# One graph layer: the ends of the transformer layers, layer 0's queries and the last group in a new order

## Chip, cores, metric

The kernel runs on one core of a Trainium2 chip, as one launch. The metric is the device time in microseconds; the time of a kernel is the median of its runs. TensorE is called PE here (PEld: its weight loads), VectorE DVE, ScalarE ACT, GpSimd POOL, and SyncE SP, which starts most of the transfers.

## What is computed

6250 nodes of 256 features, 106,250 edges of 64 features, all in float32. After a LayerNorm, the nodes go through two branches that are added to x; then a routed block of 32 small experts is added, each node by the one expert with the highest router value.

```python
xn = layernorm(x)
# branch 1: a graph network
agg = segment_sum(edge_attr, src) / max(count, 1)
g = relu(concat([xn, agg, u]) @ gW1 + gb1) @ gW2 + gb2
# branch 2: four layers with linear attention, 8 heads of 32
for i in range(4):
    h = layernorm(y) * g1 + b1                     # y starts as xn
    q = softmax(h @ Wq * s, over the 32 of a head)
    k = softmax(h @ Wk * s, over all 6250 nodes)
    context = einsum('nd,ne->de', k, h @ Wv)       # per head
    y = y + (q @ context) @ Wo + bo
    h = layernorm(y) * g2 + b2
    y = y + gelu(h @ W1 + c1) @ W2 + c2            # 256 -> 1024 -> 256
x = x + g + y
z = layernorm(x)
e = argmax(z @ router_w.T + router_b)
out = x + relu(relu(z @ W1[e] + b1[e]) @ W2[e] + b2[e])
```

## The kernel before

**Tiles and groups.** Nodes lie in 49 tiles of 128; `group(g)` is four tiles, 512 nodes. There are NG = 13 groups; the last, group 12, has one tile of 106 nodes. X keeps all nodes in SBUF. `pairs(n)` is two tiles[...]. `bank()` (L69) hands out six banks in turn, and a bank must have been read before it is written again; the edge products have two of their own. The order of the instructions is written by hand: each engine runs its instructions in the order of the program.

**A layer's context.** The softmax of k runs over all nodes, so a layer is cut in two. First, group by group, `qk` (L410) makes the keys transposed (L419), takes the running maximum, the exponentials `ek` and their sums `l`, and then the queries, as two pairs (L453), with their softmax in `q` on DVE and ACT (L459 to L468). `context_t` (L472) transposes ek (L479) into `kt` and q (L487) into `qT`. `context` (L491) adds a group's keys times its normed nodes (L499) to `C`, rescaled by `alpha`. When all 13 groups are done, `context_out` (L514) divides C by l, transposes it (L523), multiplies by Wv (L532), keeps the diagonal heads (L535) and multiplies by Wo (L538): `M` (L539) is what a query row is multiplied with. Only then can `attn_out` (L177, product L184) of the next part begin, followed by `norm2`, `attn_out_t` (transposes through L135), `ff_in` (L202, Gelu on ACT at L212) and `ff_out` (L215).

**The loops.** Layer 0's keys and queries have a loop of their own (L550): for each group the transposes of the group before (`context_t`), two halves of the norms of later groups (`norms_b`, `norms_a`), `qk`, `context` of the group before, one step of the edges, and the transposes of the next group. Then for layers 0 to 2 a loop over the 13 groups runs the second part of layer l and the first part of layer l+1 together: `ff_in`, `attn_out_t` of the next group, `context_t` of the group before, `ff_out`, `norm1`, `context`, `attn_out` two groups ahead, `norm1_t`, `qk`, `norm2`. After the loop come `context_t` and `context` of group 12 and then `context_out`. Layer 3's second part runs in a last loop together with the graph branch (`graph_in`, `graph_hidden_t`, `graph_hidden`, `graph_out`) and the router (`choose`, `route`).

**The edges.** The sums of edge features by node are made by 208 steps (`edges`), spread over the loops by hand: a load of features and of source ids (`edge_load`, SP), a comparison on DVE (`edge_match`, L352), a product on PE (`edge_sum`, L365) and four indirect transfers with addition into four tables in DRAM by POOL (`edge_add`, L383).

**Weights.** Each of w1, w2, wqkv and wo has one buffer, loaded again for the next layer by SP when its last reader is done: `load_w1` and `load_w2` around the last group, `load_wqkv` after `context_out`. The graph branch's weights (gwx, gwe, gwu, gwo, L627 to L630) lie in SBUF that the layers' pools give back when their block ends; a product with gwu (L639) makes the graph bias before the last loop.

**Router and experts.** `route` (L754) counts the nodes of each expert and scatters the rows of a group to the expert's place in the DRAM table `xtab`, by one indirect transfer for each tile (L775) from the buffer `rows`, of which there is one. After the loop the 32 experts read their first 256 rows (`xg`, L852), and 12 further blocks of 128 rows are read by `other_load` (L936) after `blank_rows` (L923) has cleared the ends of the long lists by six indirect transfers (L925). `experts` runs 44 slots; the result of each tile is scattered to the output by POOL (`out_x`, L987), two a slot for the 32, one for each further block. After each such scatter a memset of one element (`spare`) stands on POOL; the scatters are declared free of dependences among each other.

## Time and profile before

| | us |
|---|---|
| median of three runs (2973.36 to 2979.73) | 2975.72 |
| the profiled execution's own time | 2972.65 |
| its span, first to last instruction | 2970.9 |
| granted TensorE clock, mean | 0.976 |
| layer 0, to its first ff_in product | 0 to 220.8 |
| layers' loops, to the last layer's first ff_in product | 220.8 to 2121.2 |
| last loop, with graph branch and router | 2121.2 to 2839.6 |
| experts, from their first load | 2839.6 to 2970.9 |

The profile is that of one execution; its sums are compared with that execution's own time. A page gives each engine's busy time, the span in 40 slices, the chain of work that ended last, and the costliest groups of instructions; the trace behind it answers questions about one stretch: a timeline of each engine with the idle time before an instruction and the engine that ended it, the waits of an engine, and windows with the granted clock. "L223" is line 223 of the kernel. In the chain that ended last, 87% of the span is PE, 7% DVE, 2% ACT.

### The profile page before, as it was taken

How to read it: one execution, taken by the hardware profiler on the slowest of the kernel's cores; microseconds unless marked ns; L12 is line 12 of the kernel's file. 1: busy time of each engine (PE TensorE's matmuls, PEld its weight loads, DVE VectorE, ACT ScalarE, POOL GpSimd, SP SyncE). 2: the span in 40 equal slices, each digit the busy share in tenths (PEclk: the TensorE clock that was granted, in tenths of full speed). 3: DMA queues.
4: the chain of work that ended last, by engine and by line, in shares of the span. 5: the costliest groups of instructions: out<-in, count | busy, mean ns of one | idle time of the engine just before them, and what ended most of it. 6: DMA issues, size and time to landing. Idle time of an engine off the chain costs nothing.

```text
span 2970.9 us, 36212 instructions
## 1 busy us (share of the span) xinstructions
PE 2849.9 (96%) x12594; PEld 2056.6 (69%) x12594; DVE 1536.1 (52%) x4194; ACT 1126.9 (38%) x1995; POOL 1458.1 (49%) x1108
## 2 busy tenths in 40 slices
PE   7989999999989999999899999999799999999977
PEld 5767777777766777777767777777566766765654
DVE  7874645555546464646455555544343543543453
ACT  6754343434334344343443434344223223223232
POOL 0445777777747777777746656454001001001057
PEclk9999999999989999999999999999899999999888
DMA  8234555655555555555734443231200101102152
GB/s 257 35 50 84 75 96 75 97 73 97 79 110 82 89 82 88 78 94 78 133 59 79 76 75 49 42 43 18 74 15 29 36 22 29 36 22 72 55 188 76
DMA packets 368983, 219.12 MB, mean 74 GB/s; under 512 B 265913, under 2 KB 333469, under 8 KB 368792
## 3 DMA queue, kind: packets, MB, share of 16 engines
q1 hardware_dynamic: 241832, 175.32, 22.9%
q0 software_dynamic: 126144, 40.61, 17.3%
q8 instruction: 102, 1.67, 0.2%
q14 instruction: 89, 0.73, 0.1%
q10 hardware_dynamic: 816, 0.79, 0.1%
HBM read 135.46 MB, written 85.49 MB: 74 GB/s over the span
## 4 chain that ended last, share of the span: by engine, by line
PE 87%; DVE 7%; ACT 2%; issue 2%; POOL 1%; DMA 1%; POOLq 0%; SPq 0%; ACTq 0%; DVEq 0%
PE mm L223 23%; PE mm L209 23%; PE seg L365 5%; PE mm L184 5%; PE mm L419 5%; PE mm L499 4%; PE mm L453 4%; PE mm L699 3%; PE mm L135 3%; PE mm L715 3%; PE mm L700 2%; PE mm L487 1%; PE mm L479 1%; POOL out_x L987 1%; PE mm L972 1%
## 5 line engine op out<-in xcount | busy, mean ns | idle before, releaser
L383 POOL DMA_INDIRECT tab<-s,row x831 | 1313.5, 1581 | 738.4 <-issue 352.8
L209 PE MATMUL mm<-hT,w 128*128 128x512 f32 (+1 forms) x1664 | 686.5, 570 | 5.8 <-ACT hid L212 4.0
L223 PE MATMUL mm<-w,hid 128*128 128x256 f32 (+1 forms) x3136 | 687.8, 380 | 0.0
L223 PEld LDWEIGHTS mm<-w,hid 128*128 128x128 f32 (+1 forms) x3136 | 592.5, 190 | 80.1
L209 PEld LDWEIGHTS mm<-hT,w 128*128 128x128 f32 x1664 | 301.3, 190 | 354.7 <-issue 321.9
L121 ACT ACTIVATE sd<-mv,eps 128x4 f32<-128x4 f32 (+1 forms) x117 | 34.8, 297 | 991.3 <-DVE mv L120 991.1
L225 DVE TENSOR_TENSOR X<-mm,X 128x512 f32<-128x512 f32 (+1 forms) x100 | 68.1, 681 | 632.1 <-PE mm L223 632.1
L775 POOL DMA_INDIRECT xtab<-rows,to x49 | 48.2, 984 | 643.1 <-DVE to L773 574.1
L212 ACT ACTIVATE hid<-mm,col 128x512 f32<-128x512 f32 (+1 forms) x416 | 249.1, 669 | 101.1 <-PE mm L209 98.8
L365 PEld LDWEIGHTS seg<-edge,eq 128*128 128x128 f32 x1662 | 207.2, 192 | 21.5 <-issue 17.2
L365 PE MATMUL seg<-edge,eq 128*128 128x66 f32 x1662 | 202.7, 270 | 0.0
L139 ACT ACTIVATE hT<-mm,col 128x512 f32<-128x512 f32 (+1 forms) x208 | 145.0, 748 | 142.1 <-PE mm L135 140.8
L184 PE MATMUL mm<-M,qT 128*128 128x256 f32 (+1 forms) x784 | 191.3, 400 | 2.3 <-DVE M L539 2.3
L419 PE MATMUL mm<-hT,wqkv 128*128 128x512 f32 (+1 forms) x416 | 183.5, 584 | 3.5 <-ACT hT L139 3.5
L499 PE MATMUL mm<-z,kt 128*128 128x256 f32 (+1 forms) x784 | 181.8, 385 | 0.2 <-ACT kt L481 0.2
L453 PE MATMUL mm<-wqkv,hT 128*128 128x256 f32 (+1 forms) x784 | 177.7, 379 | 0.0
L453 PEld LDWEIGHTS mm<-wqkv,hT 128*128 128x128 f32 (+1 forms) x784 | 148.4, 190 | 40.7 <-issue 22.5
L184 PEld LDWEIGHTS mm<-M,qT 128*128 128x128 f32 (+1 forms) x784 | 156.2, 201 | 27.4 <-DVE M L539 4.2
L499 PEld LDWEIGHTS mm<-z,kt 128*128 128x128 f32 (+1 forms) x784 | 147.4, 192 | 19.1 <-ACT kt L481 0.4
L135 PE MATMUL mm<-ident,z 128*128 128x128 f32 x882 | 124.8, 277 | 28.3 <-DVE z L127 16.9
L352 DVE TENSOR_TENSOR eq<-all,srcf 128x512 f32<-128x512 int32 x208 | 142.9, 687 | 3.1 <-DMA all<-in_srct 2.7
L379 DVE TENSOR_SCALAR a<-s,twice,dump 128x4 f32<-128x4 f32 x208 | 60.4, 291 | 154.4 <-ACT s L367 154.4
(209 smaller groups left out, 3310.5 us busy)
## 6 DMA issues: line engine op xcount, KB each, us to landing
all<-in_srct SPq DMA_DIRECT2D x207, 256.0 KB, 3.8
xtab<-zero SPq DMA_DIRECT2D x32, 1036.0 KB, 10.2
edge<-in_edge SPq DMA_DIRECT2D x207, 128.0 KB, 2.7
tab<-s,row POOLq DMA_INDIRECT x831, 3.3
xg<-xtab SPq DMA_DIRECT2D x32, 259.0 KB, 5.9
w<-in_w SPq DMA_DIRECT2D x8, 1024.0 KB, 13.8
tab<-zero SPq DMA_DIRECT2D x40, 162.5 KB, 4.9
tb<-tab SPq DMA_DIRECT2D x48, 130.0 KB, 4.1
```

What stands on the lines that cost most here:

```text
L135: nc.tensor.transpose(ps[:, j * P:j * P + r], z[j][:r, k * P:(k + 1) * P], ident[:r, :r])
L139: nc.scalar.activation(hT[:, k, :cnt], ps[:, :cnt], AF.Identity, bias=col[:, bcol + k:bcol + k + 1], scale=col[:, gcol + k:gcol + k + 1])
L184: nc.tensor.matmul(ps[:r, j, :], qT[:, k, c0:c0 + r], M[:, k, :], start=(k == 0), stop=(k == 1))
L209: nc.tensor.matmul(ps[:, :cnt], w[:, k, b * P:(b + 1) * P], h[:, k, :cnt], start=(k == 0), stop=(k == 1))
L212: nc.scalar.activation(hid[:, :cnt], ps[:, :cnt], AF.Gelu, bias=col[:, c:c + 1], scale=1.0)
L223: nc.tensor.matmul(ps[:r, j, :], hid[b][:, c0:c0 + r], w[:, b, :], start=(b == 0), stop=(b == NHB - 1))
L352: nc.vector.tensor_tensor(out=eq[:, :m], in0=ALL.pop(b)[:, :m], in1=srcf[:, t0:t0 + m].unsqueeze(2).to_broadcast([P, m, P]), op=ALU.is_equal)
L365: nc.tensor.matmul(ps[:, i, :], eq[:, i, :], e[:, i, :], start=True, stop=True)
L383: nc.gpsimd.indirect_dma_start(out=tabs[i], out_offset=bass.IndirectOffsetOnAxis(ap=row[:, i:i + 1], axis=0), in_=s[:, i, :DE + 1], in_off ...
L419: nc.tensor.matmul(ps[:, :cnt], w[:, k, c:c + P], h[:, k, :cnt], start=(k == 0), stop=(k == 1))
L453: nc.tensor.matmul(ps[:r, j * D:(j + 1) * D], h[:, k, (j0 + j) * P:(j0 + j) * P + r], w[:, k, :D], start=(k == 0), stop=(k == 1))
L499: nc.tensor.matmul(ps[:, b, :], kt[b][:r, j * P:(j + 1) * P], z[:r, j, :], start=(j == 0), stop=(j == n - 1))
```

## The change

- `qk` is split into `keys`, `queries` (one pair each) and `queries_norm`, and `context_t` into `keys_t` and `queries_t`. `keys` calls a function `then` after the ek exponentials and before the sums of l.
- Layer 0: the queries of the group before are transposed after the key product of the group, no longer before it; the loop runs over 12 groups, and group 12 is written out behind it.
- The loop of a layer runs over 12 groups. Group 11 makes only its keys in it. Group 12 is written out behind it: its `ff_in`, the key transposes and queries of group 11, `ff_out` with the bias added ahead, `norm1`, the context of group 11 in two halves, the keys and one query product of group 12.
- `context_last` replaces `context` of group 12 and `context_out`: C is scaled by alpha and 1/l before the last product is added, the steps go by half on banks of their own, one half's copies on ACT and one on DVE, and M is copied by ACT. Two transposes of queries are called in its gaps (`fill`).
- `attn_out_first` replaces `attn_out` and `norm2` of group 0 in layers 0 to 2: the bias is added before M is there, and the statistics run pair by pair. The last layer keeps the old functions.
- `ff_in` of a group of one tile puts four products into one bank.
- Group 12 uses buffers of other names: its hT1 lies in an "hT2" tile and its q in a "z2" tile.
- The pools of the graph branch wait for freed bytes tile by tile (`reuse_waits="tile"`); the first loads of x and of the tables stand ahead of the four graph weights on SP, and the graph bias is made after `ff_out` of group 0.
- The last loop runs over 12 groups; behind it group 12's steps are nested with the router of group 11, and a group of one tile has a "rows1" buffer.
- `blank_rows` declares its transfers free of dependences among each other, puts a memset of one element behind each, and is called at slot 12 in place of 14.

```diff
+        def attn_out_first(l):
+            i0, n, r, t0, cnt = group(0)
+            xs = [X[:r, i0 + j0:i0 + j0 + m, :] for j0, m in pairs(n)]
+            for x2 in xs:
+                nc.vector.tensor_tensor(out=x2, in0=x2, in1=BO[l][:r].unsqueeze(1).to_broadcast([r, 2, D]), op=ALU.add)
...
+            for (j0, m), x2 in zip(pairs(n), xs):
+                ps = bank().rearrange("p (j d) -> p j d", j=2)
+                for j in range(m):
+                    c0 = t0 + (j0 + j) * P
+                    for k in range(2):
+                        nc.tensor.matmul(ps[:r, j, :], qT[:, k, c0:c0 + r], M[:, k, :], start=(k == 0), stop=(k == 1))
+                nc.vector.tensor_tensor(out=x2, in0=ps[:r, :m, :], in1=x2, op=ALU.add)
+                for j in range(j0, j0 + m):
+                    nc.vector.bn_stats(out=st[:r, j, :], in_=X[:r, i0 + j, :])
+                    nc.vector.bn_aggr(out=mv[:r, j, :], in_=st[:r, j, :])
...
+            m = 4 if n == 1 else 1
+            for b0 in range(0, NHB, m):
                 ps = bank()
...
-            def context_out(l):
+            def context_last(l, fill):
...
+                for b in range(2):
+                    nc.vector.tensor_scalar(out=C[:, b], in0=C[:, b], scalar1=alpha[:, b:b + 1], scalar2=rl[:, b:b + 1],
+                                            op0=ALU.mult, op1=ALU.mult)
+                ps = [bank()[:, :D] for _ in range(2)]
+                for b in range(2):
+                    nc.tensor.matmul(ps[b], kt[b][:r, :P], Z1[g][:r, 0, :], start=True, stop=True)
+                    nc.vector.scalar_tensor_tensor(out=C[:, b], in0=ps[b], scalar=rl[:, b:b + 1], in1=C[:, b],
+                                                   op0=ALU.mult, op1=ALU.add)
...
+                for b in range(2):
+                    pt = [bank()[:, :P] for _ in range(2)]
                     for k in range(2):
+                        nc.tensor.transpose(pt[k], C[:, b, k * P:(k + 1) * P], ident)
+                    nc.scalar.activation(GT[:, 0, b * P:(b + 1) * P], pt[0], AF.Identity, bias=col[:, bc:bc + 1],
+                                         scale=col[:, gc:gc + 1])
+                    nc.vector.tensor_scalar(out=GT[:, 1, b * P:(b + 1) * P], in0=pt[1], scalar1=col[:, gc + 1:gc + 2],
+                                            scalar2=col[:, bc + 1:bc + 2], op0=ALU.mult, op1=ALU.add)
+                    if b == 0:
+                        fill[0]()
...
+                    nc.scalar.copy(M[:, b], ps[:, :D])
+                fill[1]()
...
-            for g in range(NG):
+            for g in range(NG - 1):
                 if g:
-                    context_t(g - 1)
...
+                    keys_t(g - 1)
+                norms_b(g + 1)
...
+                def rest():
+                    if g:
+                        queries_t(g - 1)
+                    queries(0, g, 0)
+                    queries(0, g, 1)
+
+                keys(0, g, then=rest)
+                for i in range(2):
+                    queries_norm(g, i)
...
+            def last_steps(l):
+                g = NG - 2
+                queries_t(g, (0,), between=lambda: keys_t(g + 1))
+                context_last(l, (lambda: (queries_norm(g + 1, 0), queries_t(g, (1,))), lambda: queries_t(g + 1)))
...
+                ff_in(l, g + 1)
+                edges(2)
+                load_w1(n)
+                ff_bias(l, g + 1)
+                keys_t(g)
+                queries(n, g, 0)
+                queries(n, g, 1)
+                queries_norm(g, 0)
+                ff_out(l, g + 1, bias=False)
+                load_w2(n)
+                norm1(g + 1)
+                queries_norm(g, 1)
+                context(g, (0,))
+                norm1_t(n, g + 1)
+                context(g, (1,))
+                keys(n, g + 1, then=lambda: queries(n, g + 1, 0))
...
+                last_steps(n)
...
-            gw = gs.enter_context(tc.tile_pool(name="gw", bufs=1))
-            gp = gs.enter_context(tc.tile_pool(name="gp", bufs=1))
+            gw = gs.enter_context(tc.tile_pool(name="gw", bufs=1, reuse_waits="tile"))
+            gp = gs.enter_context(tc.tile_pool(name="gp", bufs=1, reuse_waits="tile"))
...
+            graph_load(0)
+            nc.sync.dma_start(out=gwx, in_=gw1[0:D, :].rearrange("(k p) h -> p k h", p=P))
...
-                rows = gp.tile([P, 4, XROW], F32, name="rows", bufs=1)
+                rows = gp.tile([P, n, XROW], F32, name="rows" if n > 1 else "rows1")
...
+            g = NG - 1
+            ff_in(l, g)
+            graph_in(g)
+            graph_out(g - 1)
+            graph_hidden_t(g)
+            ff_out(l, g)
+            graph_hidden(g)
+            choose(g - 1)
+            graph_out(g)
+            route(g - 1)
+            choose(g)
+            route(g)
...
+            tc.declare_no_dep(st.ins, group="blank", reason="rows of other experts")
+            tc.add_to_no_dep_group("blank", st.ins)
+            nc.gpsimd.memset(spare, 0.0)
...
-        elif s == 14:
+        elif s == 12:
             blank_rows()
```

## The prediction

> **What bounds the kernel.** I read the page's busy shares first, then PE's waits, then PE's timeline wherever it is not dense.

> ```profile
> PE 2849.9 (96%) x12594; PEld 2056.6 (69%) x12594; DVE 1536.1 (52%) x4194; ACT 1126.9 (38%) x1995; POOL 1458.1 (49%) x1108
> ...
> PEclk9999999999989999999999999999899999999888
> ```

> PE is busy 96% of 2970.9 us, so inside the layers' loops (one group of 512 nodes every 50.15 us, no gap in the timeline) an edit can win nothing. What can be won lies between the loops: the end of each layer's context, layer 0, and the router and experts at the end. PE's timeline at the end of the first full layer:

> ```profile
> 830.72 0.47 PE L479 MATMUL mm<-ident,ek 128*106 128x128 f32 x2
> 833.46 0.62 PE L487 MATMUL mm<-ident,q 106*128 106x106 f32 x2 [2.27 <-DVE q L468]
> 833.87 1.95 PE L499 MATMUL mm<-z,kt 106*128 106x256 f32 x4
> 837.67 1.09 PE L523 MATMUL mm<-ident,C 128*128 128x128 f32 x4 [1.85 <-DVE C L521]
> 839.47 2.10 PE L532 MATMUL mm<-kt,wqkv 128*128 128x128 f32 x8 [0.71 <-ACT kt L527]
> 842.09 2.07 PE L538 MATMUL mm<-wo,ek 128*128 128x256 f32 x4 [0.52 <-DVE ek L535]
> 844.94 9.55 PE L184 MATMUL mm<-M,qT 128*128 128x256 f32 x32 [0.78 <-DVE M L539]
> 855.77 1.64 PE L135 MATMUL mm<-ident,z 128*128 128x128 f32 x8 [1.27 <-DVE z L127]
> 857.84 2.41 PE L209 MATMUL mm<-hT,w 128*128 128x512 f32 x5 [0.43 <-ACT hT L139]
> ```

> Columns: start, duration, line, shapes, in brackets the idle time before it. For the last group (106 nodes) almost nothing but a chain runs: q normalized (2.27 idle), context, C scaled (1.85), transposes, V, heads, Wo, M (0.78), the attention product, the norm (1.27). Also, the same products take longer than elsewhere: 32 of L184 take 9.55 us, against 3.67 for 16 inside the loop. The granted clock, in windows of the same trace (us, busy PE, PEld, DVE, ACT, POOL, then PEclk):

> ```profile
> 832.70:849.80 17.10, 12.48 (x34) 9.03 (x35) 5.60 (x15) 2.89 (x6) 12.39 (x8) 0.50 0.84 183
> 203.40:206.80 3.40, 1.26 (x7) 0.70 (x6) 1.67 (x5) 0.92 (x2) 2.79 (x3) 1.00 0.34 18
> ```

> PE ran at half clock for 17.1 us there; in layer 0's end, where two products kept running through the gaps, it did not. Layer 0 and the last layer's start, from the waits:

> ```profile
> PE mm L487 <- DVE q L468: 20.0, 15, 2.3
> ...
> PE mm L639 <- DMA gwu<-in_gw: 5.7, 1, 5.7
> ```

> **The sum, part by part.** All durations are of the profiled execution.

> 1 *Layer boundary, twice (808.24 and 1445.74).* From the last key product of group 11 to the first ff_in product of the next layer is 857.84 - 808.24 = 49.6 us; the products in it, at full-clock durations of the loop, sum to 32.2. So 17.4 are waits and slow clock. The new order, walked from 808.24: ff_in of group 12 3.7 (in two banks instead of eight, so the 1.18 wait for ACT at L209 has no cause), edge products 2.5, key transposes 0.87, queries of group 11 3.45, ff_out 3.45, half the context 1.73: 824.05. The norm (add 0.42, stats 0.6, sqrt 0.3, scale 0.4, after ff_out's end at 822.3) is ready at 824.5, so 0.4 of wait; then transposes 0.2, half context 1.73, keys 0.92, query 0.86: 828.35. Now the chain: DVE and ACT for the key softmax end at 829.1, key transposes and copy 0.7, C scale on DVE until 830.8, product 0.43 and add 0.45 twice: 831.7; transposes 0.2 and copies 0.3 (ACT and DVE, a half each), with queries_norm's 1.1 on DVE in between, so that DVE's second half is done only at 833.4; V 0.43, heads 0.25, Wo 0.43, copy on ACT: M at 835.2. In the gaps run the query transposes (0.43, 0.18), which PE had before the chain. attn_out_first: two pairs 3.45, DVE add 0.7 and stats 1.1 for the second, sqrt 0.35, recip 0.2, first z 0.4..1.4, transposes, hT 0.7: ff_in at about 843.6, that is M + 8.4; attn_out(1) (3.45) lies beside it. 843.6 - 808.24 = 35.4. **14.2 us each, 28.4 for two.** The 128x256 copy on ACT has no row of its own; it lies between half of L481's (0.54 of a 1.08 pair, hence 0.3) and a whole one (0.54); I take 0.35. Behind that copy on ACT stand only the query copies (0.4), for which only attn_out of group 12 waits, 500 us later. The BO add now precedes M on DVE, under Wo.

> 2 *End of layer 0.* The same chain at full clock is 25.25 us today (195.59 to 220.84). New: keys 0.87, query 0.86, context of group 11 3.45, chain as above 14.9: 20.1. **5.2.**

> 3 *Layer 0.* Each group waits 1.1 us for q before L487; PE's work is 13.8 of 15.13. But DVE is nearly as full:

> ```profile
> 114.29 0.16 DVE L443 TENSOR_TENSOR l<-l,alpha 128x2 f32<-128x2 f32 x1 [0.24 <-ACT alpha L429]
> 115.62 0.16 DVE L444 TENSOR_TENSOR l<-l,ks 128x2 f32<-128x2 f32 x1 [1.18 <-ACT ek L439]
> ```

> DVE idles 1.42 of 15.13. The new order puts queries before the two sums of l, so both waits are covered by q's reductions; in exchange the q exponentials stand behind two qT copies (1.07) on ACT and DVE waits about 0.3 for them. Period 14.1, DVE-bound. It counts only from the edge match at 62.40, which waits for a load ("all", issued at 53.61 behind the 40 table clears on SP) and so stays put: eight periods, **7.4** (bounds 0 and 11).

> 4 *Last layer's start.* 2067.41 to 2121.16 is 53.75, with no edge products and 5.69 of wait for gwu. Chain as in 1 less 2.6 of edges: M 24.3 after 2067.41, then the old attn_out(0) with norm2: M + 10: 34.3. The graph bias (8 products, 1.84 at half clock, 0.9 at full) moves behind ff_out. **18.5.** The four graph weights now stand behind graph_load(0) on SP: they are used at L699, 58 us after their issue today (2103 to 2161.69), and the five loads now ahead of them take SP 4.6 us; hidden. The table read is 35 us ahead of use, too. The stall after ff_in(0) (2.33 + 1.27, DVE waiting for a sqrt behind eight Gelus on ACT) stays.

> 5 *Router of the last groups.*

> ```profile
> 2818.04 3.73 PE L715 MATMUL mm<-gwo,gh 128*106 128x256 f32 x8
> 2828.37 0.61 PE L135 MATMUL mm<-ident,z 106*128 106x106 f32 x2 [6.60 <-DVE z L127]
> ```

> The 6.60 wait holds 3.46 of DVE waiting for the four scatters that read the only "rows" buffer. With rows1 and with graph_out(12) ahead of route(11), graph_out ends near 2814.6 instead of 2821.8 (at full clock: hidden 3.7 from 2805.3, with 1.1 of wait for aT). But route(11) is then no earlier (2819.3 by DVE's order), its four scatters hold POOL until 2824.6, and the last scatter goes at 2824.8 instead of 2833.14. **8.3**, less an even chance of a half-clock window (1.7): 7.5, bounds 2 (half clock all through, as now) and 8.5.

> 6 *Blank rows.* The experts' part is a chain of scatters on POOL, 1.28 apart; six blanks break it:

> ```profile
> 2883.86 0.97 POOL L925 DMA_INDIRECT xtab<-blank,rows_i  x1 [0.16 <-issue]
> 2886.22 0.97 POOL L925 DMA_INDIRECT xtab<-blank,rows_i  x1 [1.40 <-DMA xtab<-blank,rows_i]
> ...
> 2898.17 0.97 POOL L987 DMA_INDIRECT out_x<-o,tok  x1 [0.30 <-issue]
> ```

> 14.3 us for six. With a memset between and no wait for landing they cost 6 x 1.28 = 7.7: **6.6**. Bounds 0 (a wait for xtab's reads stays) and 6.6. At slot 12 instead of 14 POOL gets there near its 22nd scatter; the 32 xg loads before it are landed by then (issued until 2861.8).

> Free edits: one edge call less in layer 0 (213 in all, 209 needed); clears of xtab spread over 36 slots, needed 32, and the first scatter comes after the last; load_w1 as before follows ff_in(12) on SP. w1 takes 13.8 us to land and is needed at 843.6: issued near 816, it has 13 us to spare; w2, issued near 823 and needed 14 us after w1, 20; wqkv waits for the V products as before.

> **Sum** 28.4 + 5.2 + 7.4 + 18.5 + 7.5 + 6.6 = 73.6. The profiled execution took 2972.65 (span 2970.9 and 1.75 around it), giving 2899; the median shown is 3.07 above it, so **2902 us**.

> [...]half of the 12.48 us busy at 0.50, 6.2 per boundary, would stay, and parts 1 and 4 would bring 28.3 in place of 46.9. The second window above speaks for me: 1.26 us of work, 0.4 of it transposes, kept 1.00; the new chain has at least 0.86 of real products in any 3.4 us.

> **Rivals.**
> - *The clock drops in the new chain as well*: three times 6.2, and 6 in the router: 2902 + 24.6 = 2927. For it: the window of 829.3 to 832.7 lost it with 0.57 of wide products. Chance 0.2.
> - *The side parts do nothing*: DVE stays at 15.1 (7.4), blanks still wait (6.6), the router's scatters hold the end (7.5): 2923. Chance 0.13.
> - *Slower: w1 late.* On SP, w1 stands behind the loads of three edge calls in a row, which wait for edge products; such a wait has lasted up to 27.5 us. One of them from 812.8 puts the issue at 840.3 and ff_in 10.5 late, at two boundaries: 2923. Break-even is 37 us late: two waits in a row (812.8 + 55 + 13.8 = 881.6, 38 late twice) give 2978, no change; three give 65.5 twice, 3033. Against it: those products are issued at 814 themselves. Chance of slower 0.05, of no change 0.02.
> - *Forecast*: 0.60, own range 2890 to 2913 (parts 5 and 6 at their bounds, and the half-clock windows in the last layer's loop, six of 1.7 us today, falling otherwise).

> Range 2886 to 2934: low end the forecast with layer 0 at 11 and fewer such windows; high end past the two middle rivals. 0.2% (6 us) is what a measurement can tell: faster 0.93 (the first two rivals and the forecast are on that side), same 0.02, slower 0.05.

> **What would show it.** L549 with no wait on q in layer 0, period 14.1; first L241 of a layer 35 us after the last L459 of group 11; clock 1.00 across it; no wait for gwu; the last scatter to xtab 35 us after the last group's first ff_in product, not 43.75; POOL's blanks 1.28 apart. A long wait of L241 for w1, or 0.50 behind the chain, would refute me.

## The result, and the profile after

| | before | after | predicted |
|---|---|---|---|
| median, us | 2977.72 (4 runs, 2973.36 to 2981.24) | 2930.26 (4 runs, 2925.60 to 2930.91) | 2902 (2886 to 2934) |
| profiled execution, us | 2972.65, span 2970.9 | 2930.91, span 2929.1 | |
| mean granted clock | 0.976 | 0.983 | |

The ratio of the runs is 0.9838, 95% interval 0.9820 to 0.9856: 47 us faster. The profiled executions differ by 41.8 us, where the sum of the prediction was 73.6. The time is inside the range, but in its upper end, and the shortfall of 31.8 us has to be found. The span, cut at the same places in both traces:

| stretch | before | after | won | predicted |
|---|---|---|---|---|
| layer 0, to its first ff_in product (parts 2 and 3) | 220.84 | 213.52 | 7.3 | 12.6 |
| boundary 1, last key product of group 11 to the next ff_in | 49.6 | 44.9 | 4.7 | 14.2 |
| boundary 2 | 49.9 | 44.0 | 5.8 | 14.2 |
| boundary 3 (part 4) | 53.75 | 34.96 | 18.8 | 18.5 |
| last loop, first ff_in of group 0 to that of group 12 | 668.2 | 672.7 | -4.5 | 0 |
| router, to the last scatter into xtab (part 5) | 43.75 | 40.36 | 3.4 | 7.5 |
| first scatter of the output to the end (part 6) | 120.5 | 113.9 | 6.7 | 6.6 |
| all the rest | | | -0.4 | 0 |

The 18.5 of part 4 already charge 0.9 for the graph bias, which this cut puts into the last loop: for boundary 3 alone the prediction walked to 34.3 us.

The page of after, busy time and the granted clock in 40 slices, has PE's share only one point higher (96% to 97%):

```profile
PE 2838.0 (97%) x12594; PEld 2050.6 (70%) x12594; DVE 1540.5 (53%) x4202; ACT 1131.2 (39%) x2006; POOL 1463.0 (50%) x1114
...
PEclk9999999999999999999999999999999999999989
```

**Boundary 1.** PE's timeline of after (start, duration, line, shapes, idle before it):

```profile
817.32 2.66 PE L566 MATMUL mm<-z,kt 128*128 128x256 f32 x8 [2.33 <-ACT kt L538]
823.67 0.59 PE L135 MATMUL mm<-ident,z 106*128 106x106 f32 x2 [3.69 <-DVE z L127]
...
836.80 3.73 PE L204 MATMUL mm<-M,qT 128*128 128x256 f32 x16
```

The two waits, 6.0 us, stand ahead of the chain, where the prediction had nothing but products one behind the other (and 0.4 of wait for the norm). From M on it goes nearly as predicted: L204 to the first ff_in is 8.9 us (predicted 8.4). Who holds `kt`? ACT's timeline over the same time:

```profile
808.54 0.38 ACT L406 COPY s<-seg 128x264 f32<-128x264 f32 x1 [1.23 <-DMA tab<-s,row]
816.40 0.38 ACT L406 COPY s<-seg 128x264 f32<-128x264 f32 x1 [7.48 <-DMA tab<-s,row]
816.68 1.08 ACT L538 COPY kt<-mm 128x512 f32<-128x512 f32 x2
```

ACT stood for 7.48 us before the copy of an edge sum, because the buffer `s` of four steps earlier was still being read by POOL's scatters (1.85 us each, four a step). The key transposes' copies, whose input had been ready since 808, are the next instructions in ACT's queue; the exponentials of q come behind them (819.07), DVE waits for those, and PE for both. The windows (us, then busy PE, PEld, DVE, ACT, POOL, then the clock, the DMA share and GB/s) add the second price:

```profile
818.50:828.70 10.20, 6.51 (x20) 5.00 (x19) 5.79 (x14) 5.34 (x8) 8.68 (x6) 0.50 0.49 77
828.70:845.70 17.00, 15.69 (x80) 11.82 (x78) 13.35 (x40) 6.96 (x20) 8.43 (x6) 1.00 0.47 98
```

The half clock falls on the stall and is over before the chain; the chain itself runs at 1.00. Boundary 3, where no edge steps are left, has neither wait.

**Layer 0.** PE no longer waits for q at its transposes (L549), but DVE's wait for the load of `all` has grown from 2.7 to 8.2 us in all, 6.79 of it in one place, with PE waiting 6.20 us behind it (L566 at 70.66) and half clock for 6.8 us from 67.6 (a half-clock window; the shortest last 3.4 us):

```profile
62.90 0.69 DVE L391 TENSOR_TENSOR eq<-all,srcf 128x512 f32<-128x512 int32 x1 [6.79 <-DMA all<-in_srct]
```

After it the period is 14.53 us (15.13 before, 14.1 predicted). **The router** has two waits that the prediction's sum charged with 1.1 in all:

```profile
2773.38 0.69 PE L818 MATMUL mm<-xT,gwx 128*128 128x106 f32 x4 [1.24 <-ACT xT L137]
2775.11 0.47 PE L819 MATMUL mm<-aT,gwe 64*128 64x106 f32 x2 [1.04 <-DVE aT L808]
```

and half clock from 2777.8 to 2788.0, under the router's products of group 11 and the graph products of group 12. **The blank rows** do what was forecast; POOL's timeline shows six at 1.28 us, 7.67 in all, in place of 14.3:

```profile
2843.55 0.97 POOL L1053 DMA_INDIRECT xtab<-blank,rows_i  x1 [0.15 <-issue]
2844.83 0.97 POOL L1053 DMA_INDIRECT xtab<-blank,rows_i  x1 [0.21 <-issue]
...
2851.22 0.97 POOL L1119 DMA_INDIRECT out_x<-o,tok  x1 [0.15 <-DVE z L1083]
```

### The profile page after: what moved, and what is told of

It reads as the page before. It is cut to its first block, busy times and chain, and to the rows that moved or that the text cites. A ratio compares the mean times of both kernels' runs of the same rounds, so it can differ in the third digit from the quotient of the medians.

```text
span 2929.1 us, 36216 instructions
## 1 busy us (share of the span) xinstructions
PE 2838.0 (97%) x12594; PEld 2050.6 (70%) x12594; DVE 1540.5 (53%) x4202; ACT 1131.2 (39%) x2006; POOL 1463.0 (50%) x1114
## 3 DMA queue, kind: packets, MB, share of 16 engines
q8 instruction: 102, 1.67, 0.2%
## 4 chain that ended last, share of the span: by engine, by line
PE 87%; DVE 4%; POOL 3%; ACT 2%; DMA 2%; issue 1%; POOLq 0%; ACTq 0%; SPq 0%; DVEq 0%
PE mm L241 23%; PE mm L261 23%; PE seg L404 6%; PE mm L184 5%; PE mm L566 5%; PE mm L459 5%; PE mm L500 4%; PE mm L135 4%; PE mm L818 3%; PE mm L834 3%; POOL out_x L1119 2%; PE mm L819 2%; PE mm L536 1%; PE mm L549 1%; PE mm L856 1%
## 5 line engine op out<-in xcount | busy, mean ns | idle before, releaser
L241 PE MATMUL mm<-hT,w 128*128 128x512 f32 (+1 forms) x1664 | 686.8, 571 | 1.7 <-ACT hT L139 1.7
L241 PEld LDWEIGHTS mm<-hT,w 128*128 128x128 f32 x1664 | 303.3, 191 | 349.4 <-issue 325.7
L404 PE MATMUL seg<-edge,eq 128*128 128x66 f32 x1662 | 202.4, 270 | 0.0
L139 ACT ACTIVATE hT<-mm,col 128x512 f32<-128x512 f32 (+1 forms) x208 | 144.9, 747 | 142.7 <-PE mm L135 140.3
L566 PE MATMUL mm<-z,kt 128*128 128x256 f32 x768 | 182.9, 392 | 14.5 <-DVE q L510 10.6
L459 PE MATMUL mm<-hT,wqkv 128*128 128x512 f32 (+1 forms) x416 | 182.4, 582 | 3.1 <-ACT hT L139 3.1
L184 PE MATMUL mm<-M,qT 128*128 128x256 f32 (+1 forms) x736 | 178.0, 397 | 0.0
L566 PEld LDWEIGHTS mm<-z,kt 128*128 128x128 f32 x768 | 146.1, 195 | 37.9 <-PE mm L500 7.4
L184 PEld LDWEIGHTS mm<-M,qT 128*128 128x128 f32 (+1 forms) x736 | 145.4, 199 | 21.7 <-ACT M L622 0.2
L135 PE MATMUL mm<-ident,z 128*128 128x128 f32 x882 | 125.1, 279 | 27.5 <-DVE z L127 15.9
```

The source lines that it names most:

```text
L135: nc.tensor.transpose(ps[:, j * P:j * P + r], z[j][:r, k * P:(k + 1) * P], ident[:r, :r])
L139: nc.scalar.activation(hT[:, k, :cnt], ps[:, :cnt], AF.Identity, bias=col[:, bcol + k:bcol + k + 1], scale=col[:, gcol + k:gcol + k + 1])
L184: nc.tensor.matmul(ps[:r, j, :], qT[:, k, c0:c0 + r], M[:, k, :], start=(k == 0), stop=(k == 1))
L241: nc.tensor.matmul(part[i], w[:, k, b * P:(b + 1) * P], h[:, k, :cnt], start=(k == 0), stop=(k == 1))
L404: nc.tensor.matmul(ps[:, i, :], eq[:, i, :], e[:, i, :], start=True, stop=True)
L459: nc.tensor.matmul(ps[:, :cnt], w[:, k, c:c + P], h[:, k, :cnt], start=(k == 0), stop=(k == 1))
```

## The experiments

Each is an edit of the changed kernel, and is given as a ratio to the kernel before on the same chip (the changed kernel: 0.9838). Its stretches are read in its own trace. On the chip of four of them (the two with fewer edge steps, the later loads, the graph pools) the experts' part took 19 to 21 us longer, and the kernel before was 17 us slower in all; the reason was not found, and so only ratios and stretches compare.

### One edge step less ahead of a boundary, then two

```diff
-share = ((2, 1, 1, 1) if g + 2 == NG or (l + 2 == DEPTH and g < 6)
+share = ((2, 1, 1, 0) if g + 2 == NG else (2, 1, 1, 1) if l + 2 == DEPTH and g < 6
...
 ff_in(l, g + 1)
-edges(2)
+edges(1)        # in the second kernel only
```

> The changed kernel with one edge step less ahead of each of the first two layer boundaries (the last of group 11, share[3] = 0; the step is made later in the next layers). THEORY (the copy of the edge sums on ACT waits 7.48 us for POOL's scatters, and the key transposes' copies, the queries' exponentials and with them PE stand behind it): no wait over 1.5 us on that copy between 800 and 830, no wait of PE over 1.5 us before the chain, clock 1.00 there, boundary (last key product of group 11 to first ff_in product) 33 to 37 us in place of 44.9 and 44.0; in all 15 to 24 us faster than the changed kernel (2906 to 2915). RIVAL (the chain drops the clock and waits by itself, as the second reading of the prediction had it): only the edge product of 1.0 us goes from each boundary; 0 to 3 us faster (2927 to 2930), clock 0.5 for 7 to 10 us as now.

> The changed kernel with two edge steps less at each of the three boundaries: share[3] = 0 at group 11, and one step in place of two behind the ff_in of group 12. THEORY (a burst of three steps overruns the four buffers of edge sums; two fit): the second step less brings only its own product, 1.0 us a boundary, so 1 to 4 us faster than with one step less, and the same clock. RIVAL (POOL is behind for the whole loop, the depth of the burst matters little): each step taken away brings the same, so that the first brings some 4 us a boundary and the second 4 again.

Measured: ratio 0.9805 (0.9786 to 0.9824) and 0.9785 (0.9768 to 0.9801). Boundaries 1 and 2: 44.9 and 44.0 with three steps in a row, 39.1 and 35.1 with two, 34.2 and 34.2 with one. ACT's timeline with two, then ACT's and PE's with one:

```profile
811.53 0.38 ACT L406 COPY s<-seg 128x264 f32<-128x264 f32 x1 [4.07 <-DMA tab<-s,row]
```
```profile
807.00 0.43 ACT L406 COPY s<-seg 128x264 f32<-128x264 f32 x1
807.26 1.14 ACT L538 COPY kt<-mm 128x512 f32<-128x512 f32 x2
```
```profile
815.59 0.37 PE L135 MATMUL mm<-ident,z 106*128 106x106 f32 x2 [0.54 <-DVE z L127]
```

With one, the copy of the edge sums no longer waits, `kt` comes 9.4 us earlier, and the clock is 1.00 across both boundaries. That ACT's wait for POOL's scatters was the cause is shown: at boundary 1 it is 7.48, 4.07 and 0 us long, and the boundary shrinks with it. The edits take the whole edge step away; one that leaves it in place (more buffers `s`, or the copy behind those of `kt` on ACT) was not tried. The expectation that two steps fit held at boundary 2, where the first step taken brought nearly all, and was wrong at boundary 1: with two the copy still waits 4.07 us and the clock is lost for 3.4 us. So the first edit won some 10 us by the ratios, not 15 to 24. Two products of 1.0 us were moved away from each boundary; the other 8 us of each are wait and clock. With one step in a row the boundary is 34.2. The prediction walked to 35.4 with three edge products in it; less two of them (0.87 each in the trace of after, an estimate) that is 33.7. (Boundary 3 became 36.4, since the last two edge products, 1.8 us, fall into it.)

### The weights' loads later in layer 0

```diff
 clear_tabs()
-load_wo(0); load_bo(0); load_w1(0); load_w2(0)
...
     elif g:
         edges()
+    if g == 3:
+        load_wo(0); load_bo(0); load_w1(0); load_w2(0)
```

> The changed kernel with layer 0's loads of wo, bo, w1 and w2 (2.5 MB, issued from 49.5 to 53.3) put behind the edge step of group 3. THEORY (the comparison of edges at 62.90 waits 6.79 us for a load that stands behind these on SP and shares the transfers with them; DVE holds PE's context product for 6.2 us and that costs the clock for 6.8 us): wait before that comparison under 2 us, PE's longest wait before L566 under 1.5 us, no half-clock window at 67, first ff_in product at 205 to 208 in place of 213.5, 5.5 to 9 us faster (2921 to 2925). RIVAL (the 40 table clears, 6.5 MB, and not the weights, hold the load): 0 to 3 us faster, wait 4 to 7 us.

Measured: first ff_in product at 205.2, ratio 0.9821 (0.9805 to 0.9838). PE's wait at group 2's context product is 0.48 in place of 6.20:

```profile
64.19 3.69 PE L566 MATMUL mm<-z,kt 128*128 128x256 f32 x16 [0.48 <-DVE q L510]
```

and there is no half-clock window in layer 0. The theory holds, 8.3 us of stretch: it was the order on SP and the 2.5 MB that travelled ahead, not the table clears, which stay where they were. The ratio alone, with its interval, would not have settled it.

### The query transposes of layer 0 back in their old place

On top of the kernel just told; the queries stay ahead of the sums of l.

```diff
-    keys_t(g - 1)
+    context_t(g - 1)
...
     def rest():
-        if g:
-            queries_t(g - 1)
         queries(0, g, 0)
```

> The kernel with the weights' loads later in layer 0 (first ff_in product at 205.2, undisturbed), and in it the query transposes of layer 0 put back ahead of the key product; the queries stay ahead of the sums of l. THEORY (the later transposes give the shorter period): PE waits again about 1 us a group for q, period 14.9 to 15.2 us in place of 14.5, first ff_in product at 208 to 211. RIVAL (the sums of l, which no longer hold DVE ahead of the queries, give it): period within 0.15 of 14.5, first ff_in product at 205 to 206.5.

Measured: ratio 0.9789 (0.9773 to 0.9805), first ff_in product at 203.1, and both theories missed: the period, read between context products,

```profile
107.80 3.62 PE L566 MATMUL mm<-z,kt 128*128 128x256 f32 x16
121.73 2.54 PE L566 MATMUL mm<-z,kt 128*128 128x256 f32 x11
```

is 13.9 us, PE without any wait. (Of the ratio some 5 us are the last loop's, 667.1 us here, with fewer half-clock windows.) DVE has lost the waits of 0.24 and 1.18 us that the kernel before has at the two sums of l:

```profile
110.45 0.15 DVE L485 TENSOR_TENSOR l<-l,alpha 128x2 f32<-128x2 f32 x1
110.70 0.16 DVE L486 TENSOR_TENSOR l<-l,ks 128x2 f32<-128x2 f32 x1
```

But for the later loads, the order of this loop differs from that of the kernel before in these two sums alone. So the gain in period, 15.13 to 13.9, comes from them, now behind the queries' maxima and subtractions on DVE, and the transposes a product later *cost* 0.6 us a group. Not all of that reaches the stretch: in its first two groups the old order waits 1.44 and 1.17 us for q, has a half-clock window from 31.0, and is 4.2 us longer there, so that 2.1 us are left. In the changed order PE waits 0.48 us a group at L566 for DVE, and DVE 0.52 for the square root on ACT (L318); in the old order neither wait is there. Which of the changed instructions closes that ring (the bank that the context product gets, or the q copies on ACT) was not tried.

### Less work for DVE in layer 0

```diff
-nc.vector.tensor_scalar(out=X[:r, i0 + j, :], ...)
+eng = nc.gpsimd if g > 3 and j > 1 else nc.vector
+eng.tensor_scalar(out=X[:r, i0 + j, :], ...)
```

> The kernel with the weights' loads later in layer 0, and in it two of the four scalings of X a group (L315, 0.34 us each on DVE) given to POOL from group 4 on. THEORY (the period of layer 0, 14.5, is DVE's: 13.7 busy and 0.5 of wait): PE's wait of 0.48 at the context product goes, period 13.9 to 14.2, first ff_in product 2.5 to 4.5 us earlier (201 to 203). RIVAL (the sqrt on ACT and its table load, or a slower and later scaling on POOL, hold DVE instead): period 14.4 or more, first ff_in product at 205 or later.

Measured: first ff_in product at 242.6, 37 us later; ratio 0.9929 (0.9913 to 0.9946). On POOL one scaling took 1.79 us (0.41 on DVE), and stood behind four scatters in POOL's queue; the period became 20.0. Busy time and mean ns of one, between 90 and 200 us:

```profile
L316 POOL TENSOR_SCALAR X<-X,mv,rs 128x256 f32<-128x256 f32 x11 | 16.8, 1791 | 0.0
```

The rival was right and the miss is large. It says nothing against DVE as the limit: it put a longer chain in its place.

### The chain without its fillings

On top of two edge steps less.

```diff
 def last_steps(l):
-    context_last(l, (lambda: (queries_norm(g + 1, 0), queries_t(g, (1,))), lambda: queries_t(g + 1)))
+    context_last(l, None)
+def late_steps():     # called in attn_out_first ahead of the z2 tiles; behind the chain for the last layer
+    queries_norm(g + 1, 0); queries_t(g, (1,)); queries_t(g + 1)
```

> The kernel with two edge steps less at each boundary (boundaries of 34.1, 34.1 and 36.3 us at full clock there), and the two fillings of the chain taken out of it: the query transposes of groups 11 and 12 run behind attn_out_first in the first two boundaries and behind the chain in the third. THEORY (the fillings, though transposes, keep the clock): the granted clock drops to 0.5 for 7 to 20 us behind the chain, boundaries 1 and 2 are 4 to 9 us longer, in all 8 to 20 us slower than with the fillings (ratio to before 0.981 to 0.986). RIVAL (the products that are left and gaps of under 1 us keep it[...]): clock 1.00 across, boundaries within 1.5 us of those with the fillings, in all 0 to 3 us slower (ratio 0.9785 to 0.980).

Measured: ratio 0.9818 (0.9798 to 0.9838), boundaries 38.4, 37.0 and 36.1. By the time this looks like the theory; by the trace it is not. In the chain the clock is 1.00 without fillings, at all boundaries, and the chain is 0.8 us shorter (from the last key product of group 11 to L204 24.5 us, 25.3 with fillings). What is lost comes behind it, where I put the filling: PE waits for q's norm, which stands on DVE behind the wait for another norm's square root.

```profile
840.16 0.61 PE L550 MATMUL mm<-ident,z 106*128 106x106 f32 x2 [3.15 <-DVE z L522]
...
1465.97 0.40 PE L550 MATMUL mm<-ident,z 106*128 106x106 f32 x2 [3.15 <-DVE z L522]
```

The same wait cost 3.4 us of half clock at boundary 1 and none at boundary 2 (the last section has an estimate of why). Layer 0's end has it too, with half clock, and is 25.1 us in place of 20.6. So the fillings are worth 3 to 4.5 us at each of these places as work that finds an idle place, and nothing as keepers of this chain's clock.

### The graph branch's pools

```diff
-gw = gs.enter_context(tc.tile_pool(name="gw", bufs=1, reuse_waits="tile"))
+gw = gs.enter_context(tc.tile_pool(name="gw", bufs=1))        # and gp alike
```

> The changed kernel with the graph branch's pools waiting as a whole again (reuse_waits taken out of gw and gp), all else as changed. THEORY (the wait for the graph weights went because the bias product stands behind ff_out of group 0 and the chain ends 19 us earlier, not because of waits tile by tile): first load of x issued 0 to 6 us later than 2073.7, no wait of PE for it, time 2928 to 2932. RIVAL (the tile-wise waits carry it): loads after the last reader of the block, x and tables late for graph_in of group 0 (its transposes at 2103.7), 4 to 10 us slower (2934 to 2940).

Measured: ratio 0.9843 (0.9827 to 0.9860), boundary 3 34.96, no wait of PE for gwu; the first load of x was issued at 2074.78 (2073.68 in the changed kernel). So the tile-wise waits bring nothing here. Whether the place of the bias product or the earlier end of the chain took the wait away was not separated. The last loop took 667.4 us in this run, 5.3 less than in the changed kernel with the same instructions: it had four half-clock windows of 3.4 us where the other had seven.

### The router's two halves taken apart

```diff
 ff_out(l, g)
-if g: choose(g - 1)
+if g: choose_t(g - 1)         # the 8 transposes of z
 if g + 2 < NG:
     attn_out(l, g + 2)
+if g: choose(g - 1)           # the 16 products of 32 columns, and DVE's part
```

> The changed kernel with the router's transposes and its 16 products of 32 columns taken apart in the last loop: attn_out of the group two ahead stands between them. THEORY (these two together fill 3.3 us[...] and cost the 3.4 us half-clock windows, 7 of them in the last loop in the changed kernel and 4 in one whose loop is the same but begins at another time): no 3.4 us window between 2130 and 2740, last loop (first ff_in of group 0 to that of group 12) 660 to 663 us in place of 672.7 (667.4 to 672.7 in kernels with the same loop), 5 to 12 us faster. RIVAL (the windows come from the whole stretch of graph transposes, router and weight loads): windows stay at 4 to 7, loop 667 to 673, within 3 us of the changed kernel.

Measured: ratio 0.9769 (0.9749 to 0.9789), last loop 650.7 us, 22.0 less than in the changed kernel, and no half-clock window between 2130 and 2740. The gain was underestimated. PE's timeline of the changed kernel, then of this one:

```profile
2346.86 1.04 PE L135 MATMUL mm<-ident,z 128*128 128x128 f32 x8
2348.19 2.24 PE L856 MATMUL mm<-rw,zT 128*128 128x32 f32 x16 [0.29 <-ACT zT L137]
```
```profile
2346.19 3.62 PE L184 MATMUL mm<-M,qT 128*128 128x256 f32 x16
2349.64 1.87 PE L865 MATMUL mm<-rw,zT 128*128 128x32 f32 x16
2351.35 1.96 PE L818 MATMUL mm<-xT,gwx 128*128 128x512 f32 x4
```

With attn_out between, the copies of zT are done when the small products start. From the first transpose to the product behind the small ones (L184 at 2350.26) were 3.40 us; now the two parts take 0.88 (2345.31 to 2346.19) and 1.71 (2349.64 to 2351.35). That is 0.8 for each of 11 groups, 9 us; seven windows at 1.7 us are another 12 (an estimate). Measured, transposes and 32-column products side by side, 3.4 us, lost the clock in seven groups; apart they lose it in none. It is not the moment at which the loop begins: the two later kernels with this edit have no such window either, and the changed kernel and the eight others without it have four to seven each (the kernel before six, the changed one seven). The last section has an estimate of how much other work stood beside them where the clock was kept.

### Group 12's graph inputs ahead of the router's norm

```diff
 def graph_out(g, between=None):
...
+    if between is not None: between()
     layernorm(small, n, r, lambda j: rows[:r, j, :D], ...)
...
-graph_out(g - 1)
-graph_hidden_t(g)
+graph_out(g - 1, between=lambda: graph_hidden_t(g))
```

> The changed kernel with the transposes of group 12's graph inputs, and their copies on DVE and ACT, put ahead of the router norm of group 11 (graph_hidden_t called inside graph_out, ahead of its layernorm). THEORY (PE waits 1.24 and 1.04 us at 2773 and 2775 for these copies, which stand behind the norm on both engines, and these two gaps cost the clock from 2777.8): no wait over 0.3 us there, no half-clock window that begins before the products with rw (L856) are done, last scatter to xtab 34 to 37 us behind the first ff_in product of group 12, in place of 40.4: 3 to 7 us faster. RIVAL (short products and transposes drop the clock there with or without the gaps): 37.5 to 39.5 us, only the gaps' 1 to 2.5 us are won.

Measured: router 33.3 us in place of 40.36, ratio 0.9819 (0.9799 to 0.9838). Both waits are gone,

```profile
2774.17 0.59 PE L818 MATMUL mm<-xT,gwx 128*128 128x106 f32 x4
```

and the clock holds until 2786.8, 26.9 us after group 12's first ff_in product (20.1 in the changed kernel); so it does in the two later kernels with this edit (26.6 and 27.0), and in none of the nine without it (they lose it after 17.1 to 20.1). Theory confirmed, 7.0 us: 2.3 of gaps and 4.7 of what they drew after them.

### All together

> Two edge steps less at the boundaries, the weights' loads later in layer 0, the graph transposes ahead of the router norm in group 12, and the router's transposes apart from its products: four edits at once on the changed kernel. THEORY (each takes away a stall of its own): the gains add up, 16 (boundaries) + 8 (layer 0) + 3 to 7 (router) + 5 to 12 (last loop) = 32 to 43 us faster than the changed kernel, ratio to before 0.969 to 0.973. RIVAL (windows of half clock and waits move elsewhere): 20 to 25 us, ratio 0.975 to 0.977.

Measured: 2875.79 us, ratio 0.9655 (0.9638 to 0.9672): 54 us below the changed kernel, more than the 43 expected, since the last loop won 22. The stretches add up: layer 0 205.9, boundaries 34.2, 34.2 and 36.4, last loop 650.8, router 33.3. Two stalls were left. For the first, the query transposes went back to their old place in layer 0, as above; for the second:

```diff
+graph_norm(0)                # x's norm for the graph branch, taken out of graph_in(0)
 norm2(1)
```

> The four edits together (ratio 0.9655), and two more: layer 0's query transposes back ahead of the key product (period 13.9 in place of 14.5), and the norm of group 0's x for the graph branch made ahead of the first ff_in of the last layer instead of behind it (PE waits 2.27 and 1.18 us for it behind eight Gelus, and the clock is 0.5 for 6.8 us from 2077). THEORY (both stalls are on the path): first ff_in product at 203 to 204 in place of 205.9, last loop 643 to 646 us in place of 650.8, no half-clock window in it; 6 to 10 us faster than the four edits, ratio 0.962 to 0.9635. RIVAL (the norm ahead delays the Gelus and with them PE by as much): 1 to 3 us faster, last loop 649 or more.

Measured: **2866.50 us, ratio 0.9615 (0.9602 to 0.9628)**, first ff_in product at 202.4, last loop 643.7, and no half clock between 33 and 2725: as in the theory, with the ratio just past its range. This version beats both kernels, the changed one by 66 us by the ratios.

## Why the prediction was right, and where it was not

The direction was right, and so was the main mechanism as a whole: in the new order the end of a context is about as short as walked, wherever nothing stalls ahead of it. Which share of that the halves, the earlier bias and the separate banks have, no run separates; the fillings are not what shortens the chain, which is 0.8 us shorter without them. The range held, in part by luck: the forecast's own 2890 to 2913 missed, and the range went on to 2934 for two rivals that did not come true as they stood. The most likely time was 28 us too low, by the following steps.

1. **"Edge products 2.5 ... 824.05", part 1: the step that failed.** The walk charged an edge step with its product on PE and took ACT as free. A step also has a copy on ACT that must wait for POOL, and the new order put three steps in a row ahead of it, at about 7.4 us of POOL each. The prediction did look at what stands behind the edge calls on SP (the w1 rival; w1 was issued at 807.35 and never waited for), but not at ACT. Instead of 14.2 each, 4.7 and 5.8 were won: 17.9 us of the shortfall of 31.8. With one step the boundary is 34.2 us (33.7 by the walk), so the rest of the walk stands, and so does part 4, which had no edge steps: 34.96 us for 34.3. The walk's sums have slips that change little: its terms give 823.9 and 824.0 where it has 824.05 and 824.5 (the latter made its 0.4 of wait), and part 2 takes the chain at 14.9 where part 1 has 15.25.
2. **End of layer 0**: 25.25 to 20.6; predicted 20.1. Right.
3. **"It counts only from the edge match ... eight periods", part 3.** Two terms were wrong. The match at 62.40 did not stay a neutral anchor: what came earlier on DVE now waits longer for the same load, PE with it, and the clock goes. And the period was not 14.1 but 14.53. Of 7.4 us 2.7 were won (eight periods of 1.03 us less would have been 8.2; the sum has a slip there). Besides, the cause was put down wrongly in part: the moved transposes cost time, the moved sums of l win it.
4. **Graph weights**: no wait, as predicted; but by the place of the bias product or the earlier chain, not by the waits tile by tile.
5. **"at full clock: hidden 3.7 from 2805.3", part 5.** The products ran at half clock from 2777.8. The forecast took less than one half-clock window of loss (7.5 of 8.3) and had 2 as its lower bound; 3.4 came. The two gaps that cost the clock were in the sum as 1.1 us of wait.
6. **Blank rows**: POOL's six are 6.6 us shorter, as predicted, and the stretch 6.7.
7. **The last loop**, taken as unchanged, lost 4.5: 0.95 for the bias product, which moved into it (charged in part 4), and, by an estimate, 3.4 for 34.1 us at half clock in place of 27.3.

Of the rivals, "the clock drops in the new chain as well" gave 2927, near the measured 2930, but for another reason: the chain kept the clock, and the stall ahead of it lost it. "The side parts do nothing" was wrong for the blanks. And the argument that the fillings hold the clock was not needed: the chain holds it without them, and no run shows whether they would. The window of 203.4 to 206.8 that spoke for them says little, too: a border of the grid in the last section, 204.7, runs through it, and PE is busy for 2.06 and 2.20 us of the two stretches beside that border.

## What to carry to other kernels

Before moving a block of work to a spot where one engine is free, list every instruction that it puts on the other queues and what each one waits for; a copy of 0.38 us on ACT held a chain for some 9 us because a slow queue on another engine released its buffer. Where transposes and narrow products stand together and the trace shows half clock behind them, try a dense product between (here the 3.62 us of attn_out): taking two such blocks apart brought more than any single part of the change, 9 of its 22 us by hiding copies. And when several edits go in together, undo them one at a time in the trace, since one of them may cost what another wins.
